# Residual additions of a top-k graph layer and a Mamba layer: from VectorE to identity products in PSUM with ScalarE evictions

## The chip, the cores and the metric

The kernel runs on one core of a Trainium2 chip. The metric is device time in microseconds (us) of one launch. TensorE is written PE (its weight loads PEld), VectorE DVE, ScalarE ACT, GpSimd POOL; SP is the queue from which nearly all DMAs are issued.

## What is computed

x has shape (8, 256, 48, 48): 8 images, 256 channels, 2304 tokens. Two layers follow each other, each with a residual addition around it:

```
x = x + L0(groupnorm(x))     # tokens @ W.T + bias -> feat, pos; pos normalized;
                             # sim = pos pos^T; per token the 16 largest, softmax,
                             # weighted mean of their feat rows
x = x + L1(groupnorm(x))     # two Mamba blocks in a row: layernorm, in-projection,
                             # causal conv of 4 taps, silu, step sizes by softplus,
                             # h = h * exp(dt*A) + dt*B*x (16 states, 512 channels),
                             # y = C.h + D*x, y * silu(z), out-projection
```

These two "x +" are what the change is about. All data are fp32.

## The kernel before, in words

**Layouts.** A chunk is T = 384 tokens; there are NCH = 6 of them in an image, and TB = 3 blocks of 128 tokens in a chunk, so 18 blocks in an image. Activations lie with channels on the 128 partitions (CB = 2 halves of 256 channels).

**The scan sets the order of everything.** A *unit* is one chunk of one Mamba block (depth d = 0 or 1), so there are 12 units in an image and 96 in all; their order within an image, from `order`, is (chunk, depth) = (0,0) (1,0) (2,0) (0,1) (3,0) (1,1) (4,0) (2,1) (5,0) (3,1) (4,1) (5,1), numbered 0 to 11 here. A unit has 16 steps of two parts, so 32 *hooks*; one hook m holds one DVE scan over 770 elements (`run_scan`, L943). For each hook ACT makes two exponentials into one of two PSUM buffers (`decay`, L928). For each step POOL makes the scan's input for all four state groups, 128x1536 (`make_bx`, L907). After the scan its states are multiplied with C either by POOL, once a step for all the parts that fall to it (`pool_part`, L971, issued at the first hook of the next step, 128x1536 for two parts or 128x768 for one), or by DVE at once (L945). Which part goes where is written out by hand in `SHARE`, a string of 32 letters (G for POOL, V for DVE), one string for each of three stages: the middle of an interleaved image (units 1 to 9), its edges (units 0, 10, 11), and the last image. PE then sums the states (`sum_states`, L989).

**Everything else hangs on hooks.** The tables `between`, `behind` and their `_spare` and `_last` forms give for each function of a unit the hook, counted from the unit's first scan, at which it is issued, ahead of that hook's scan (`inner`) or behind it (`outer`). A function of unit u at hook 38 therefore falls in unit u + 1, hook 6. The output projection (`out_proj`, L1005) is at 37 and 38, and `leave` (L1012) at 38 to 40: at depth 0 it copies the projection out of PSUM on ACT (L1020) and stores it; at depth 1 it adds bias and residual on DVE (L1024) and stores the result. The residual was fetched into `res` by `load_out` at hook 33 (L1002).

**Layer 0 of the next image runs between.** `layer0` is a generator. For image 0 it runs alone, before the first scan; for the others `Ahead.go` takes one step of it at each hook, from hook EARLY = -21 before the image's start. First come about 49 steps of projections (`project`, `features`, `norms`, `normalized`, `scale`), then the 18 blocks, 16 hooks apart, whose start is held to a fixed place modulo 16 (L1152). The list `within` (L560) gives the place of each function of a block: similarities on PE, eight largest twice on DVE (`top`), exponentials on ACT, the weighted mean on PE, `average` (22), `turn_back` (24), which transposes the 128x256 result into PSUM with two products by the identity, and `finish` (24), in which DVE adds the transposed result to x (L551). After each third block DVE takes statistics of the chunk and it is stored as x1. The chunk of x for this addition is loaded in `average` of the chunk's first block (L537), into a rotating tile, tag "x", three deep; `load_out` and the projections take their tiles from the same tag.

Each engine works through its instructions in the order in which they are written here, and SP issues its DMAs in that order too, so an instruction or a store that waits holds what is behind it.

The two additions, as they were:

```
nc.vector.tensor_add(xr, xr, row["pr"].rearrange("p (k t) -> p k t", k=CB))        # L551
nc.vector.scalar_tensor_tensor(                                                    # L1024
    res[:, cb, :], unit["pw"][cb], b_feat[:, cb : cb + 1], res[:, cb, :], ALU.add, ALU.add)
```

Of the kernel before, what the change touches and what calls it, by code (L numbers as in the profile page):

```python
# [11 lines left out]
AF = mybir.ActivationFunctionType  # L12
ALU = mybir.AluOpType
# [3 lines left out]
P = 128  # L17
# [9 lines left out]
def tile_conv_preact(  # L27
# [18 lines left out]
    nc = tc.nc  # L46
# [5 lines left out]
    CB = C // P  # L52
# [19 lines left out]
    FOLDED = (2, 3,)  # L72
    EARLY = -21


    SHARE = (
        "GGVGGGVGGGVVGVGGGGGVGGGVGGGGGVVG",
        "GVGGGVVVGGVVGGGGVGGVGGVVVGVVGVGV",
# [8 lines left out]
    def load_chunk(pool, src, c, tag, name, bufs):  # L87
        t = pool.tile([P, CB, T], F32, tag=tag, name=name, bufs=bufs)
        nc.sync.dma_start(t, src[:, c * T : (c + 1) * T].rearrange("(k p) t -> p k t", p=P))
        return t  # L90
# [170 lines left out]
    def layer0(b, left, pool, ps0, alone):  # L261
# [229 lines left out]
        def invert(t):  # L491
            nc.vector.reciprocal(blocks[t]["den"], blocks[t]["den"])

        def others(t, i):
# [36 lines left out]
        def average(t):  # L531
            row = blocks[t]
            row["o"] = pool.tile([P, C], F32, tag="o", name=f"o_{b}_{t}", bufs=more)
            nc.scalar.activation(row["o"], row["po"], AF.Identity, scale=row["den"])
            if t % TB == 0:
                tag, bufs = ("xr", 2) if alone else ("x", 3)
                rows[t // TB] = load_chunk(pool, x[b], t // TB, tag, f"xr_{b}_{t}", bufs)  # L537

        def turn_back(t):
            row = blocks[t]  # L540
            row["pr"] = mm0(C, f"pr_{b}_{t}")
            for cb in range(CB):
                nc.tensor.transpose(
                    row["pr"][:, cb * P : (cb + 1) * P], row["o"][:, cb * P : (cb + 1) * P], ident
                )

        def finish(t):
            row = blocks[t]
            c, j = divmod(t, TB)
            xr = rows[c][:, :, j * P : (j + 1) * P]  # L550
            nc.vector.tensor_add(xr, xr, row["pr"].rearrange("p (k t) -> p k t", k=CB))  # L551
            if j + 1 == TB:
                xr = rows.pop(c)
                for cb in range(CB):
                    nc.vector.bn_stats(st1[:, cb, c, :], xr[:, cb, :])
                nc.sync.dma_start(x1[:, c * T : (c + 1) * T].rearrange("(k p) t -> p k t", p=P), xr)
            row.clear()
# [5 lines left out]
            (16, weigh, 0), (1, top, 1), (-9, similar, 0), (-7, similar, 1), (-7, similar, 2), (22, average),  # L563
            (-6, similar, 3), (-7, keep_similar, 1), (-3, keep_similar, 3), (-1, top, 0),
            (-3, keep_similar, 4), (15, turn, 1), (10, others, 4), (5, others, 0), (3, top, 2), (6, add_top),
# [438 lines left out]
    def out_proj(unit, cb):  # L1004
        pw = unit["pw"][cb] = mm(T, f"pw_{unit['u']}_{cb}")  # L1005
        for k in range(DB):
            nc.tensor.matmul(  # L1007
                pw, unit["ow"][:, k, cb * P : (cb + 1) * P], unit["z"][k],
                start=(k == 0), stop=(k == DB - 1),
            )  # L1010

    def leave(unit, cb):  # L1012
# [9 lines left out]
        else:  # L1022
            res = unit["res"]
            nc.vector.scalar_tensor_tensor(  # L1024
                res[:, cb, :], unit["pw"][cb], b_feat[:, cb : cb + 1], res[:, cb, :], ALU.add, ALU.add
            )
# [25 lines left out]
        (-3, load_rep, "dt", 1), (-29, load_in, 2), (5, in_proj, 7), (-20, tap, 0), (-15, taps, 1),  # L1052
        (-2, load_rep, "dtx", 3), (38, leave, 1), (22, load_rep, "dtx", 15), (-8, load_in, 4), (-37, mean),
        (-19, taps, 0), (5, load_d, 1), (-19, in_proj, 1), (-10, load_bc, 0), (-30, root_end),
        (-9, times_x, 0), (29, gate, 2),
    ]
    between_spare = [
        (25, sum_states, 2), (-34, variance), (-21, in_proj, 0), (38, out_proj, 0), (-15, taps, 2),
        (-35, square), (39, leave, 0), (23, load_rep, "dt", 14), (5, load_rep, "dt", 5),
# [8 lines left out]
        (7, load_rep, "dt", 6), (17, load_rep, "dt", 12), (-6, load_rep, "dtx", 1), (-14, load_in, 7),  # L1068
        (37, gate, 3), (-31, root), (9, load_rep, "dt", 7), (5, load_d, 1), (-24, load_in, 3),
        (17, load_rep, "dt", 11), (14, load_rep, "dtx", 11), (-13, x_proj), (-17, load_in, 6), (-3, load_d, 0),  # L1070
# [8 lines left out]
        (-2, load_rep, "dtx", 3), (8, copy_z, 1), (22, load_rep, "dtx", 15), (-16, load_in, 4), (-38, mean),  # L1079
        (-22, normal), (-37, center), (-21, in_proj, 1), (-12, load_bc, 0), (-30, root_end), (-9, times_x, 0),  # L1080
        (-25, load_in, 1), (-28, scale),
# [9 lines left out]
        (-17, tap, 1), (21, load_rep, "dt", 13), (-20, tap, 0), (-10, step_size, 1), (-5, load_rep, "dt", 0),  # L1091
        (9, copy_z, 2), (-18, in_proj, 2), (2, load_rep, "dtx", 5), (10, sum_states, 0),
        (13, load_rep, "dt", 9), (33, gate, 2), (-2, in_proj, 4), (9, silu_z), (7, load_rep, "dt", 6),
# [125 lines left out]
```

## Time and profile before

| | |
|---|---|
| median of three runs | 9424.92 us (9422.48 to 9425.63) |
| the profiled execution | 9422.82 us |
| its span, first to last instruction | 9421.1 us |
| first scan begins, last scan ends | 468 us, 9409.5 us |
| mean granted PE clock | 0.898 |
| L551, DVE addition in layer 0 | 144 of 407 ns |
| L1024, DVE addition at depth 1 | 96 of 606 ns |
| L1020, ACT copy at depth 0 | 96 of 473 ns |
| L943, DVE scan | 3072 of 1750 ns |
| L907, POOL product | 1536 of 3462 ns |
| L971, POOL product | 669 of 3190 ns (two parts), 648 of 1697 ns (one) |

A group row of the profile gives the line in the kernel, the engine, the operation, out<-in by the program's names, the shapes, the count, the busy time and the mean of one in ns. A row of waits gives who waited (engine, tile, line) for whom, the sum in us, how often, and the longest. A window row gives its bounds, its length and, for each engine, busy time and number of instructions, then the granted PE clock, the DMA share and GB/s. A busy PE is not PE at its peak, since its products overlap.

### The profile page before, as it was taken

What the parts mean: (1) busy time and instruction counts of PE and PEld (TensorE: products, weight loads), DVE (VectorE), ACT (ScalarE), POOL (GpSimd) and SP (SyncE); (2) the same over time, 40 slices, a digit from 0 to 9 for tenths busy, and PEclk for the clock granted to TensorE, in tenths of its full rate; (3) what the DMA queues carried; (4) which work ended last, traced back from release to release, by engine and by line L of the source; (5) the groups of instructions that cost most, each with busy time, mean ns of one, the idle gap of its engine ahead of it and who ended that gap; (6) DMA issues with size and microseconds to landing.
All of it is one profiled execution on the core that took longest, in us unless ns stands there. A gap on an engine that the chain in (4) does not pass through costs nothing. (4 is left out here: it accounts for less than half of the span.)

```text
span 9421.1 us, 120485 instructions
## 1 busy us (share of the span) xinstructions
PE 7867.0 (84%) x37049; PEld 4423.6 (47%) x37049; DVE 8867.3 (94%) x7543; ACT 7307.1 (78%) x16242; POOL 8867.9 (94%) x3605
## 2 busy tenths in 40 slices
PE   8888987888878898798878988788887888877676
PEld 6644544455544554455444545445554455433332
DVE  6599999999989999899999999999999999989999
ACT  4578877788778877787878787778877788777776
POOL 2199999999999999999999999999999999999999
PEclk9989998899989998899988999889998899988877
DMA  4134444444444444444444434443444344444443
GB/s 128 50 123 136 134 137 152 129 136 137 136 151 129 133 140 131 151 131 139 131 144 138 140 128 140 145 138 127 138 134 157 122 141 132 138 153 145 149 147 126
DMA packets 1029829, 1275.91 MB, mean 135 GB/s; under 512 B 106529, under 2 KB 998945, under 8 KB 1028417
## 3 DMA queue, kind: packets, MB, share of 16 engines
q1 hardware_dynamic: 1028640, 1268.21, 42.0%
q8 instruction: 296, 4.85, 0.2%
q14 instruction: 349, 2.85, 0.1%
q10 hardware_dynamic: 544, 0.00, 0.0%
HBM read 1050.77 MB, written 217.06 MB: 135 GB/s over the span
## 5 line engine op out<-in xcount | busy, mean ns | idle before, releaser
L907 POOL TENSOR_TENSOR bx<-BC,dtxr 128x1536 f32<-128x1536 f32 x1536 | 5307.1, 3462 | 33.0 <-PE y L989 30.4
L928 ACT ACTIVATE da<-dtr,A_sb 128x385 f32<-128x385 f32 x6144 | 3592.8, 585 | 928.3 <-DVE bx L943 601.8
L943 DVE TENSOR_TENSOR_SCAN bx<-da,bx 128x770 f32<-128x770 f32 x1986 | 3423.7, 1746 | 85.1 <-ACT da L928 78.7
L971 POOL TENSOR_TENSOR bx<-bx,BC 128x1536 f32<-128x1536 f32 (+1 forms) x1317 | 3233.3, 2455 | 103.7 <-DVE bx L943 91.6
L943 DVE TENSOR_TENSOR_SCAN da<-da,bx 128x770 f32<-128x770 f32 x1086 | 1903.4, 1753 | 125.5 <-ACT da L928 123.1
L527 PE MATMUL po<-feat,aT 128*128 128x256 f32 x5184 | 1378.8, 415 | 236.6 <-ACT dt L842 107.3
L698 PE MATMUL pe<-vn,inw 128*128 128x384 f32 (+1 forms) x2976 | 1175.7, 524 | 216.0 <-ACT vn L775 100.6
L527 PEld LDWEIGHTS po<-feat,aT 128*128 128x128 f32 x5184 | 1022.0, 205 | 633.9 <-ACT aT L516 167.4
L456 PE MATMUL psim<-pos 128*128 128x512 f32 x2520 | 1203.2, 619 | 130.6 <-DVE xr L551 85.4
L989 PE MATMUL y<-bx,sel 128*32 128x384 f32 x12288 | 1221.6, 527 | 72.7 <-POOL bx L971 72.4
L945 DVE TENSOR_TENSOR bx<-da,BC 128x768 f32<-128x768 f32 x1086 | 1040.6, 958 | 37.4
L698 PEld LDWEIGHTS pe<-vn,inw 128*128 128x128 f32 x2976 | 567.6, 201 | 648.0 <-ACT vn L775 125.1
L456 PEld LDWEIGHTS psim<-pos 128*128 128x128 f32 x2520 | 504.4, 209 | 709.8 <-issue 385.3
L989 PEld LDWEIGHTS y<-bx,sel 128*32 128x32 f32 x12288 | 400.5, 117 | 866.6 <-issue 683.2
L803 DVE SCALAR_TENSOR_TENSOR xc<-pe,cw,xc 128x384 f32<-128x384 f32 x1080 | 655.4, 612 | 33.2 <-ACT xc L794 7.8
L516 ACT ACTIVATE aT<-pt 128x512 f32<-128x512 f32 (+1 forms) x720 | 387.7, 547 | 330.9 <-PE pt L508 328.6
L1007 PE MATMUL pw<-z,ow 128*128 128x384 f32 x1536 | 551.0, 505 | 57.5 <-ACT aT L516 38.5
L507 PE MATMUL pt<-ident,sim 128*128 128x128 f32 x2592 | 540.1, 289 | 13.4 <-DVE v L762 5.6
L986 PE MATMUL y<-xc,dmat 128*128 128x384 f32 x768 | 380.7, 581 | 157.7 <-DMA dmat<-diag 43.7
L499 ACT ACTIVATE rest<-left,three 128x512 bf16<-128x512 f32 (+1 forms) x720 | 453.5, 669 | 64.6 <-DVE left L484 64.6
L508 PE MATMUL pt<-minus,rest 128*128 128x128 bf16 x2592 | 496.1, 225 | 3.0 <-ACT rest L499 3.0
L959 ACT COPY h_st<-da 128x2 f32<-128x2 f32 x884 | 138.5, 157 | 419.9 <-DVE bx L945 409.2
(160 smaller groups left out, 9933.9 us busy)
## 6 DMA issues: line engine op xcount, KB each, us to landing
dtxr<-dtx_d SPq DMA_DIRECT2D x1536, 192.0 KB, 2.9
dtr<-dt_d SPq DMA_DIRECT2D x1536, 192.0 KB, 2.8
BC<-bc_d SPq DMA_DIRECT2D x192, 768.0 KB, 5.6
inw<-in_in_wT_dram SPq DMA_DIRECT2D x744, 128.0 KB, 2.5
dtx_d<-dtx SPq DMA_DIRECT2D x384, 192.0 KB, 1.9
dt_d<-dt SPq DMA_DIRECT2D x384, 192.0 KB, 2.0
ow<-in_out_wT_dram SPq DMA_DIRECT2D x96, 512.0 KB, 4.5
dmat<-diag SPq DMA_DIRECT2D x384, 64.0 KB, 2.7
```

The source lines that it names most:

```text
L456: nc.tensor.matmul(pm, pos[:, k, t * P : (t + 1) * P], pos[:, k, c0 : c0 + w], start=(k == 0), stop=(k == CB - 1),)
L507: nc.tensor.transpose(pt[:, q], row["sim"][:, r], ident)
L527: nc.tensor.matmul(row["po"], aT[:, m % PT, :], feat[:, m, :], start=(m == 0), stop=(m == NB - 1))
L698: nc.tensor.matmul(pe, w[:, k], unit["vn"][:, k, lo:], start=(k == 0), stop=(k == CB - 1))
L803: nc.vector.scalar_tensor_tensor(unit["xc"][e], unit["pe"][e][:, k : k + T], cw[:, unit["d"], e, k : k + 1], unit["xc"][e], ALU.mult, ALU.add,
L907: nc.gpsimd.tensor_tensor(bx[:, :, 1:], unit["BC"][0], unit["dtxr"][i].unsqueeze(1).to_broadcast([P, Q, T]), ALU.mult,)
L928: nc.scalar.activation(da[:, s * (1 + T) : (s + 1) * (1 + T)], unit["dtr"][i], AF.Exp, scale=A_sb[:, unit["d"], i, p * HQ + s : p * HQ + s ...
L943: nc.vector.tensor_tensor_scan(h, da, g, 0.0, ALU.mult, ALU.add)
L945: nc.vector.tensor_tensor(bx[:, :, 0:T], da.rearrange("p (q t) -> p q t", q=HQ)[:, :, 1:], unit["BC"][1][:, qs], ALU.mult,)
L971: nc.gpsimd.tensor_tensor(g[:, :, 0:T], g[:, :, 1:], unit["BC"][1][:, qs], ALU.mult)
L989: nc.tensor.matmul(y[j * G : (j + 1) * G, :], sel, unit["bx"][k * J + j][:, q, 0:T], start=False, stop=True, skip_group_check=True,)
L1007: nc.tensor.matmul(pw, unit["ow"][:, k, cb * P : (cb + 1) * P], unit["z"][k], start=(k == 0), stop=(k == DB - 1),)
```

## The change

Both additions are made in PSUM. In `turn_back` each transpose is followed by a product of the identity with the matching 128x128 piece of x, accumulated onto it; in `out_proj`, at depth 1, the four products of each half are followed by a fifth, identity times `res`. ACT then evicts the sum: a copy in `finish`, an Identity activation with the bias column in `leave`. The load of x for layer 0's addition moves from `average` (hook 22 of a block) to `invert` (hook 12). EARLY goes from -21 to -24. In SHARE's first string one V moves from step 6, second part, to step 7, first part. Single entries of the tables move by one to three hooks. The diff, cut to its core:

```diff
-    EARLY = -21
+    EARLY = -24
-        "GGVGGGVGGGVVGVGGGGGVGGGVGGGGGVVG",
+        "GGVGGGVGGGVVGGVGGGGVGGGVGGGGGVVG",
...
         def invert(t):
             nc.vector.reciprocal(blocks[t]["den"], blocks[t]["den"])
+            if t % TB == 0:
+                tag, bufs = ("xr", 2) if alone else ("x", 3)
+                rows[t // TB] = load_chunk(pool, x[b], t // TB, tag, f"xr_{b}_{t}", bufs)
...
             nc.scalar.activation(row["o"], row["po"], AF.Identity, scale=row["den"])
-            if t % TB == 0:
-                tag, bufs = ("xr", 2) if alone else ("x", 3)
-                rows[t // TB] = load_chunk(pool, x[b], t // TB, tag, f"xr_{b}_{t}", bufs)
...
                 nc.tensor.transpose(
                     row["pr"][:, cb * P : (cb + 1) * P], row["o"][:, cb * P : (cb + 1) * P], ident
                 )
+                nc.tensor.matmul(
+                    row["pr"][:, cb * P : (cb + 1) * P], ident,
+                    rows[t // TB][:, cb, t % TB * P : (t % TB + 1) * P],
+                    start=False, stop=True, skip_group_check=True,
+                )
...
-            nc.vector.tensor_add(xr, xr, row["pr"].rearrange("p (k t) -> p k t", k=CB))
+            nc.scalar.copy(xr, row["pr"].rearrange("p (k t) -> p k t", k=CB))
...
-            (-6, similar, 3), (-7, keep_similar, 1), ...
+            (-5, similar, 3), (-7, keep_similar, 1), ...
...
                 pw, unit["ow"][:, k, cb * P : (cb + 1) * P], unit["z"][k],
-                start=(k == 0), stop=(k == DB - 1),
+                start=(k == 0), stop=(k == DB - 1 and "res" not in unit),
             )
+        if "res" in unit:
+            nc.tensor.matmul(pw, ident, unit["res"][:, cb, :], start=False, stop=True)
...
-            nc.vector.scalar_tensor_tensor(
-                res[:, cb, :], unit["pw"][cb], b_feat[:, cb : cb + 1], res[:, cb, :], ALU.add, ALU.add
+            nc.scalar.activation(
+                res[:, cb, :], unit["pw"][cb], AF.Identity, bias=b_feat[:, cb : cb + 1]
             )
...
behind:        (-2 -> -4, load_rep, "dtx", 3)
between_spare: (-34 -> -32, variance), (-31 -> -32, root)
behind_spare:  (-30 -> -31, root_end)
between_last:  (-18 -> -21, in_proj, 2)
```

The last five rows are the moved table entries in short form, with the old and the new hook.

More of the change, by code (lines that the diff above doesn't have):

```diff
@@ L563, in layer0 @@
             (16, weigh, 0), (1, top, 1), (-9, similar, 0), (-7, similar, 1), (-7, similar, 2), (22, average),
-            (-6, similar, 3), (-7, keep_similar, 1), (-3, keep_similar, 3), (-1, top, 0),
+            (-5, similar, 3), (-7, keep_similar, 1), (-3, keep_similar, 3), (-1, top, 0),
             (-3, keep_similar, 4), (15, turn, 1), (10, others, 4), (5, others, 0), (3, top, 2), (6, add_top),
@@ L1052, in tile_conv_preact @@
         (-3, load_rep, "dt", 1), (-29, load_in, 2), (5, in_proj, 7), (-20, tap, 0), (-15, taps, 1),
-        (-2, load_rep, "dtx", 3), (38, leave, 1), (22, load_rep, "dtx", 15), (-8, load_in, 4), (-37, mean),
+        (-4, load_rep, "dtx", 3), (38, leave, 1), (22, load_rep, "dtx", 15), (-8, load_in, 4), (-37, mean),
         (-19, taps, 0), (5, load_d, 1), (-19, in_proj, 1), (-10, load_bc, 0), (-30, root_end),
@@ L1057, in tile_conv_preact @@
     between_spare = [
-        (25, sum_states, 2), (-34, variance), (-21, in_proj, 0), (38, out_proj, 0), (-15, taps, 2),
+        (25, sum_states, 2), (-32, variance), (-21, in_proj, 0), (38, out_proj, 0), (-15, taps, 2),
         (-35, square), (39, leave, 0), (23, load_rep, "dt", 14), (5, load_rep, "dt", 5),
@@ L1068, in tile_conv_preact @@
         (7, load_rep, "dt", 6), (17, load_rep, "dt", 12), (-6, load_rep, "dtx", 1), (-14, load_in, 7),
-        (37, gate, 3), (-31, root), (9, load_rep, "dt", 7), (5, load_d, 1), (-24, load_in, 3),
+        (37, gate, 3), (-32, root), (9, load_rep, "dt", 7), (5, load_d, 1), (-24, load_in, 3),
         (17, load_rep, "dt", 11), (14, load_rep, "dtx", 11), (-13, x_proj), (-17, load_in, 6), (-3, load_d, 0),
@@ L1079, in tile_conv_preact @@
         (-2, load_rep, "dtx", 3), (8, copy_z, 1), (22, load_rep, "dtx", 15), (-16, load_in, 4), (-38, mean),
-        (-22, normal), (-37, center), (-21, in_proj, 1), (-12, load_bc, 0), (-30, root_end), (-9, times_x, 0),
+        (-22, normal), (-37, center), (-21, in_proj, 1), (-12, load_bc, 0), (-31, root_end), (-9, times_x, 0),
         (-25, load_in, 1), (-28, scale),
@@ L1091, in tile_conv_preact @@
         (-17, tap, 1), (21, load_rep, "dt", 13), (-20, tap, 0), (-10, step_size, 1), (-5, load_rep, "dt", 0),
-        (9, copy_z, 2), (-18, in_proj, 2), (2, load_rep, "dtx", 5), (10, sum_states, 0),
+        (9, copy_z, 2), (-21, in_proj, 2), (2, load_rep, "dtx", 5), (10, sum_states, 0),
         (13, load_rep, "dt", 9), (33, gate, 2), (-2, in_proj, 4), (9, silu_z), (7, load_rep, "dt", 6),
```

## The prediction

> **What bounds the kernel now.** I read in this order: busy time by engine, the windows of one image cut at its 12 units (one unit is 32 scans; I took the starts of scans 0, 32, 64 ... from the timeline), the waits of POOL, and the timeline at one of them.
>
> ```profile
> PE 7867.0 (84%) x37049; PEld 4423.6 (47%) x37049; DVE 8867.3 (94%) x7543; ACT 7307.1 (78%) x16242; POOL 8867.9 (94%) x3605
> ```
>
> DVE and POOL are level at 94%, and both lose most of the rest in the first 468 us (image 0's layer 0, before the first scan), so an average cannot say which sets the pace. The windows can. Units 2 to 9 of image 3 (columns: window, its length, busy PE, PEld, DVE, ACT, POOL):
>
> ```profile
> 4255.10:4352.00 96.90, 83.77 (x409) 47.22 (x408) 95.44 (x81) 78.56 (x177) 95.03 (x36) 0.95 0.43 139
> 4352.00:4447.40 95.40, 87.58 (x412) 49.86 (x411) 94.47 (x81) 77.71 (x177) 95.40 (x36) 0.91 0.41 131
> ...
> sum 763.80, PE 675.97 PEld 384.83 DVE 755.19 ACT 619.20 POOL 759.64; mean PE 84.50 PEld 48.10 DVE 94.40 ACT 77.40 POOL 94.96
> ```
>
> In unit 5 POOL has no gap at all (95.40 of 95.40); in unit 4 it loses 1.87 us. Over the eight units POOL is idle 763.80 - 759.64 = 4.2 us, DVE 8.6. So here **POOL is the floor**, and DVE can only give back what POOL waits for it. All of that wait is one row:
>
> ```profile
> POOL bx L971 <- DVE bx L943: 91.6, 64, 3.3
> POOL bx L907 <- PE y L989: 30.4, 32, 2.6
> ```
>
> In order of time the 91.6 us lie so: units 1, 2, 4, 6, 8 of the seven interleaved images 17, 3, 12, 11 and 6, each time at hook 16 (the multiply of step 7); unit 0, 33 (hooks 13 and 22); the last image 9. The cause at hook 16 of unit 4 is to be seen ten hooks earlier, on DVE:
>
> ```profile
> 4273.70 1.14 DVE L1024 SCALAR_TENSOR_TENSOR xr<-pw,b_feat,xr 128x384 f32<-128x384 f32 x2 [0.80 <-PE pw L1007]
> 4304.10 3.17 POOL L971 TENSOR_TENSOR bx<-bx,BC 128x1536 f32<-128x1536 f32 x1 [1.87 <-DVE bx L943]
> ```
>
> The two residual additions and the wait ahead of them take 1.94 us of DVE, and POOL then waits 1.87. Unit 5, where the same place holds a depth-0 eviction on ACT, has no such wait. That pair is the experiment the change repeats.
>
> **What the Trainium skill says.** "SBUF — State Buffer", section "Who interferes with whom": a DVE instruction with at most one SBUF input does not contend with GpSimd. Both additions read one operand in PSUM, so removing them should not make POOL's own instructions shorter. The trace agrees loosely: the 128x1536 product of L907 is 3462 ns in the mean, 3442 in the last image where no L551 runs. "ScalarE: Activation LUTs", "What ACT_TABLE_LOAD costs": a pointer operand adds about 93 ns; here a 128x384 copy from PSUM takes 473 ns (L1020) and one with a bias column 575 (L369). "TensorE: Matmul & The Clock Gate", Part 2: ScalarE is strict FIFO, so an eviction that waits for PE holds the decays behind it; L1020 shows it (78.9 us in 42 waits).
>
> **The change, part by part.** Base: the profiled execution, 9422.82 us (span 9421.1 and 1.7 around it); the median 9424.92 is 2.1 above.
>
> 1. *finish* off DVE: 144 x 407 ns (L551) = 59 us of DVE gone. ACT gains 144 x 0.37 (L378, 128x256 copy from PSUM, 364 ns) = 53. PE gains two identity products a block. An fp32 product is two recorded passes (L1007: 1536 records for 96 x 2 x 4 products); a 128-column pass starts every 0.11 us (six of L446 in 0.82 against four in 0.61), so 4 x 0.11 = 0.44 a block, 64 us in all. Wait on ACT: at hook 30 PE has finished pr 3.5 us before ACT gets there; at hook 14 it ends 0.4 us after the decay, plus 0.44, so 0.85. Queued behind: the next decay and DVE's scan, which has 0.66 us to spare there; DVE is 0.41 earlier itself. Net nothing, up to 0.5 us a block; below nothing too, since PE's psim waits 85.4 us for L551 to free its bank and ACT would free it up to 5 us sooner, but PE is not the floor.
> 2. *leave* off DVE: 96 x 606 ns = 58 us, and its waits for pw, 23.6. ACT gains 96 x 575 = 55. PE gains 96 x 2 x 0.32 = 62. In units 4, 6, 8 both evictions come while out_proj is still running: ACT waits as its L1020 does in unit 5 (1.7) plus two passes, 2.4 us. Behind it are the decay of hook 8 and, on DVE, its scan; DVE has a 2.54 us MATCH_REPLACE at hook 7 to cover it, and unit 5 shows no DVE gap. If that cover went, 2.4 - 1.9 = 0.5 us a unit. In units 10, 11 and 0 PE is done 3 to 5 us early, so no wait, but 2 x 0.575 = 1.1 us of ACT work lands just before silu_z (two table loads of 1.28 and four activations), whose burst already starves DVE at hooks 10 to 13. POOL has 1.2 to 3 us in hand there in units 10 and 11 (its multiply starts that long after the scan it needs) but 0.1 in unit 0.
> 3. *SHARE*: one V moves from step 6 to step 7 of the middle stage. Counts stay (8 GG, 7 mixed, 1 VV), so POOL's sum stays. But step 6 becomes a 3190 ns multiply in place of 1697: POOL has 1.5 us more to do ahead of hook 16, where it now waits. In unit 1 (wait 2.4) it must first wait about 1.3 for the later scan of step 6; 1.1 is won.
> 4. The *xr load* moves 10 hooks earlier, past the loads of some five steps on SP's queue. It takes 3.8 us to land and its buffer (3 deep) was left long before; the identity product needs it at hook 24, 12 hooks (35 us) later. At the old place only two hooks (6 us) would remain. The *res* load leads by four hooks (12 us) against 5.2. The stores wait for ACT now, which arrives 2 to 5 us earlier than DVE did: nothing lost.
> 5. *EARLY* -24 and the table rows: layer 0's projections come three hooks sooner; the blocks keep their hooks (their start is fixed modulo 16, and at -21 they started without slack). In unit 0 two position evictions, with 2.4 us of waits for PE, move out of hooks 7 and 8, ahead of the burst. In unit 11 a 1.4 us normalization moves to hook 9, into it. From -2 to +2 us an image; I take -1.5. The single moves in the tables (root, variance, a load, an input projection) shift DMA issues and short ACT work by one to three hooks: nothing, +-5 us in all.
>
> The sum:
> - Units 1 to 9: waits of 3 + 12 + 11 + 6 = 32 us in units 2, 4, 6, 8 go, since DVE sheds 1.6 us in each unit and 1.9 more in 4, 6 and 8, ahead of the wait; unit 1 gives 7 x 1.1 = 8. 40 us at best. POOL is next late: it has nothing left to give. A tenth comes back in new waits on later decays: **-36**.
> - Units 10, 11: 0. Unit 0: 7 x (1.1 - 1.5) = **-3**.
> - Last image: POOL sits at its floor (L971's wait for scans is 9 us over 12 units) with DVE idle some 5 us a unit: 0; its tail ends in one more product and a 575 ns eviction in place of 606: **+1**.
> - The first 468 us: PE is busy 47 of 50 us in most windows, so 18 x 0.44 = 8 at most; DVE's 0.41 a block is beside the path there. **+6**.
> 9422.8 - 36 - 3 + 1 + 6 = 9391; less sure of the first term than of the rest, and with 126 us more work on a PE that is 84 to 92% busy in the middle units, I allow 5 back: 9396.
>
> **Rivals.**
> - *ACT's queue takes over (slower).* In units 4, 6, 8 ACT's added time is 2.4 + 1.1 = 3.5 against 1.9 that DVE sheds; per block 0.85 + 0.37 and 0.37 against 0.8 for the two in a unit. If every ACT delay reaches DVE's next scan and then POOL: 3 x 1.6 + 9 x 0.8 + 3 x 1.1 = 15 us an image, 105 in seven. It decides from where ACT's lag passes the 0.4 to 0.7 us that decays have in hand at hooks 14 and 30. For it: the decay is the last thing DVE waits for (202 us). Against: ACT is idle 17 to 22 us a unit, and unit 5. Half of it, less half the gain: 9423 + 52 - 18 + 7 = **9464**.
> - *The gain is given back at the image boundary.* Unit 0 loses 8 to 9 us of POOL a unit already; if its burst grows by 1.1 + 2 and unit 11's reserve of 2.5 is used up too, 7 x 4 = 28 us return: 9396 + 28 = **9424**. For it: 0.1 us in hand. Against: the waits for PE that leave hooks 7 and 8.
> - *The boundary gets better as well*: if moving the projections clears most of unit 0's POOL waits (33 + 19 us), say 25 us: **9371**.
> - *Nothing because POOL does not wait for DVE* (the releaser is inferred) is ruled out by unit 4 against unit 5.
>
> **Chances.** Forecast (9380 to 9412) 0.55; boundary better 0.13; given back 0.14; ACT takes over 0.18. About 0.2% (19 us, 9406) is what a measurement of this kernel can tell from no change. Faster: 0.13 and nine tenths of 0.55 less a little, 0.61. Same: the rest of it and 0.14, 0.20. Slower: 0.18 and the upper edge of the third, 0.19. The range runs from the better boundary to a little over the midway of the slow case: 9366 to 9445; the forecast's own is 9380 to 9412.
>
> **What would show it.** Right: the row "POOL bx L971 <- DVE" falls from 92 to some 45 us, with units 4, 6, 8 as long as 5 and 7 (95), POOL's busy time unchanged within 0.2%, DVE down by about 115 us and its waits for ACT's decays up. Wrong: POOL's gaps move to other hooks; DVE's wait for da doubles within units 2 to 9; unit 0 longer than 98 us; the first scan more than 8 us later; or POOL's products getting shorter, which I exclude.

## The result, and the profile after

| | before | after |
|---|---|---|
| median of five runs | 9425.63 us (9422.48 to 9431.65) | 9387.33 us (9386.1 to 9391.59) |
| the profiled execution, its span | 9422.82, 9421.1 us | 9387.99, 9385.9 us |
| first scan begins | 468.0 us | 476.4 us |

The ratio is 0.9959 (95% interval 0.9945 to 0.9974), 38 us less. The prediction was 9396, with a range of 9366 to 9445. The total came out as forecast. Where the gain lies did not.

Busy time by engine in the changed kernel:

```profile
PE 7960.8 (85%) x37817; PEld 4514.8 (48%) x37817; DVE 8771.5 (93%) x7303; ACT 7382.4 (79%) x16482; POOL 8867.3 (94%) x3605
```

POOL's sum is the old one (8867.9) to 0.01%; DVE has lost 96 us, ACT and PE have gained 75 and 94. In the windows of units 4, 5, 6 and 8 of image 3, cut at their scans as in the prediction (PE, PEld, DVE, ACT, POOL, then the granted clock), and the sum over units 2 to 9:

```profile
4240.85:4336.18 95.33, 85.51 (x419) 49.22 (x418) 93.76 (x78) 79.33 (x181) 94.99 (x36) 0.95 0.44 142
4336.18:4430.47 94.29, 86.19 (x425) 49.46 (x423) 93.63 (x78) 78.05 (x179) 94.29 (x35) 0.96 0.40 129
4430.47:4525.32 94.85, 85.23 (x422) 49.65 (x422) 92.96 (x75) 79.24 (x182) 94.85 (x36) 0.96 0.43 139
...
4620.20:4715.64 95.44, 87.84 (x427) 50.65 (x425) 93.80 (x77) 75.77 (x157) 95.44 (x37) 0.95 0.41 134
...
sum 761.38, PE 682.62 PEld 393.89 DVE 747.15 ACT 625.28 POOL 759.79; mean PE 85.33 PEld 49.24 DVE 93.39 ACT 78.16 POOL 94.97
```

Unit 4 was 96.90 us and is 95.33, close to unit 5. POOL is idle 1.6 us in the eight units (4.2 before), while DVE is idle 14.2 (8.6 before): DVE has become looser, POOL is the floor all the more. POOL's waits, which were 91.6 for scans and 30.4 for PE:

```profile
POOL nt_rn L176 <- ACT rn L168: 39.6, 17, 4.7
...
POOL bx L976 <- DVE bx L948: 32.1, 56, 1.9
```

The wait for scans has lost 60 us, more than forecast (to 45), but above it stands a row that the prediction has nowhere: a 9-element POOL operation that waits for ACT.

**Where the 35 us of span went.** In the loop, from the first scan to the end of the last, all that POOL does besides waiting takes 8783.5 us before and 8784.0 after. So the length of the loop is this constant and POOL's idle time, and the change can be booked by where that idle time lies. I summed the idle stretch ahead of each POOL instruction, over the seven interleaved images, by the unit in which it ends (units are cut at DVE's scans, and POOL carries work across these cuts, so neighbouring units can trade some of it):

| POOL idle, us | units 0, 1 | 2 to 9 | 10, 11 | last image | sum | POOL active | first scan |
|---|---|---|---|---|---|---|---|
| before | 89.1 | 34.7 | 24.0 | 10.0 | 157.8 | 8783.5 | 468.0 |
| after | 62.1 | 9.1 | 30.1 | 11.5 | 112.8 | 8784.0 | 476.4 |

The loop is 45 us shorter. The first stage gives 8.4 back and the tail behind the last scan 1.1: 35. Only 26 of the 45 lie in units 2 to 9, where both removed additions and the new SHARE string should act. 27 come from the two units at the start of each image, and there the windows of image 3 show it; before (units 0 and 1):

```profile
3873.09:3970.30 97.21, 79.13 (x362) 45.59 (x363) 85.58 (x77) 74.72 (x172) 88.00 (x43) 0.85 0.42 132
3970.30:4065.19 94.89, 79.59 (x340) 40.66 (x339) 93.02 (x76) 75.36 (x171) 90.37 (x34) 0.86 0.40 128
```

and after:

```profile
3861.18:3955.15 93.97, 77.13 (x352) 44.67 (x350) 84.60 (x74) 73.82 (x168) 85.22 (x37) 0.86 0.42 136
3955.15:4048.78 93.63, 79.87 (x341) 40.66 (x341) 92.67 (x76) 74.58 (x171) 93.63 (x36) 0.89 0.42 131
```

Unit 0 is 3.2 us shorter, and in unit 1 POOL now never stops (93.63 of 93.63), where it lost 4.5.

### The profile page after: what moved, and what is told of

Its sections match the earlier page's. It is cut to its first block, busy times and chain, and to the rows that moved or that the text cites. A ratio compares the mean times of both kernels' runs of the same rounds, so it can differ in the third digit from the quotient of the medians.

```text
span 9385.9 us, 121932 instructions
## 1 busy us (share of the span) xinstructions
PE 7960.8 (85%) x37817; PEld 4514.8 (48%) x37817; DVE 8771.5 (93%) x7303; ACT 7382.4 (79%) x16482; POOL 8867.3 (94%) x3605
## 5 line engine op out<-in xcount | busy, mean ns | idle before, releaser
L912 POOL TENSOR_TENSOR bx<-BC,dtxr 128x1536 f32<-128x1536 f32 x1536 | 5297.7, 3455 | 18.0 <-PE y L994 16.3
L994 PE MATMUL y<-bx,sel 128*32 128x384 f32 x12288 | 1261.1, 528 | 102.5 <-POOL bx L976 97.2
L703 PE MATMUL pe<-vn,inw 128*128 128x384 f32 (+1 forms) x2976 | 1140.7, 510 | 157.7 <-ACT vn L780 60.0
L456 PE MATMUL psim<-pos 128*128 128x512 f32 x2520 | 1124.0, 590 | 68.0 <-ACT xr L556 25.9
L950 DVE TENSOR_TENSOR bx<-da,BC 128x768 f32<-128x768 f32 x1086 | 1040.7, 958 | 37.5
L994 PEld LDWEIGHTS y<-bx,sel 128*32 128x32 f32 x12288 | 406.1, 116 | 931.0 <-issue 680.2
L703 PEld LDWEIGHTS pe<-vn,inw 128*128 128x128 f32 x2976 | 543.9, 194 | 573.8 <-ACT vn L780 79.8
L838 PE MATMUL pd<-dbl,dtp_sb 16*128 16x384 f32 x768 | 362.6, 614 | 136.3 <-DVE z L1000 66.2
```

Source lines behind the costliest of these rows:

```text
L456: nc.tensor.matmul(pm, pos[:, k, t * P : (t + 1) * P], pos[:, k, c0 : c0 + w], start=(k == 0), stop=(k == CB - 1),)
L703: nc.tensor.matmul(pe, w[:, k], unit["vn"][:, k, lo:], start=(k == 0), stop=(k == CB - 1))
L912: nc.gpsimd.tensor_tensor(bx[:, :, 1:], unit["BC"][0], unit["dtxr"][i].unsqueeze(1).to_broadcast([P, Q, T]), ALU.mult,)
L950: nc.vector.tensor_tensor(bx[:, :, 0:T], da.rearrange("p (q t) -> p q t", q=HQ)[:, :, 1:], unit["BC"][1][:, qs], ALU.mult,)
L994: nc.tensor.matmul(y[j * G : (j + 1) * G, :], sel, unit["bx"][k * J + j][:, q, 0:T], start=False, stop=True, skip_group_check=True,)
```

## The experiments

Two theories stood against each other. **DVE relief**: the gain is the prediction's first term, DVE work taken away ahead of POOL's waits. **Boundary**: it is EARLY, which moves the projections out of the way at the start of each image, and the additions themselves bring little. All runs stand here in the terms of the table above, with their ratio to the kernel before. EARLY, the depth-1 addition and the SHARE string were each tried alone and undone in the changed kernel; layer 0's addition was tried alone, and undone together with the other one (early24_share). The moved table entries were never tried apart: they are in every after_ run, in first_image_dve, one_more_v and norm_end_later, and in none of the others.

| run | units 0, 1 | 2 to 9 | 10, 11 | sum | first scan | median us | ratio (95%) |
|---|---|---|---|---|---|---|---|
| before_early24 | 51.4 | 30.5 | 34.4 | 126.2 | 468.1 | 9389.92 | 0.9961 (0.9947 to 0.9975) |
| before_finish | 88.6 | 19.1 | 21.2 | 140.1 | 476.9 | 9418.39 | 0.9990 (0.9983 to 0.9997) |
| before_leave | 96.2 | 14.5 | 22.0 | 144.2 | 471.9 | 9418.62 | 0.9992 (0.9984 to 1.0001) |
| before_share | 89.2 | 23.7 | 25.5 | 148.2 | 471.0 | 9415.78 | 0.9990 (0.9983 to 0.9996) |
| after_early21 | 86.7 | 6.2 | 19.2 | 124.0 | 477.9 | 9399.72 | 0.9972 (0.9962 to 0.9982) |
| after_early23 | 61.5 | 6.6 | 38.0 | 115.9 | 477.3 | 9395.80 | 0.9968 (0.9957 to 0.9980) |
| after_leave_dve | 53.2 | 7.7 | 30.1 | 101.1 | 477.4 | 9377.24 | 0.9949 (0.9932 to 0.9965) |
| after_old_share | 62.5 | 9.2 | 30.9 | 114.1 | 475.7 | 9394.27 | 0.9969 (0.9957 to 0.9981) |
| early24_share | 47.1 | 23.4 | 35.5 | 115.8 | 467.4 | 9384.25 | 0.9958 (0.9943 to 0.9973) |
| first_image_dve | 53.6 | 5.7 | 31.3 | 100.7 | 469.1 | 9368.99 | 0.9941 (0.9926 to 0.9955) |
| one_more_v | 64.7 | 98.9 | 30.7 | 203.8 | 468.9 | 9384.15 | 0.9958 (0.9943 to 0.9973) |
| norm_end_later | 45.3 | 8.1 | 30.4 | 93.6 | 470.5 | 9362.34 | 0.9936 (0.9919 to 0.9952) |

POOL's active time is 8782 to 8789 us in all of them but one_more_v. The stage before the first scan moves by 3 to 4 us by itself: before_share and before_leave change nothing in it. Each row of idle time is one profiled execution. The intervals are 6 to 16 us to either side, so a smaller difference between two medians is only as good as the idle time that goes with it.

### EARLY alone, and taken back

before_early24, the kernel before with one number changed:

```diff
-    EARLY = -21
+    EARLY = -24
```

> The kernel before with EARLY -24 alone. In the changed kernel -24 against -21 made unit 0 22 us shorter (seven images) while POOL waited 33 us at hook 19. If that comes from the position evictions that leave hooks 7 and 8, it shows here too: unit 0 shorter by 15 to 22 us, 9402 to 9411. If it only repairs what the eviction of depth 1 on ACT did to the burst, it gives under 5 us here: 9420 to 9426.

It takes 29.4 us off the span, and its median is within 3 us of the whole change: more than either outcome that was expected. Its windows of units 0 and 1:

```profile
3863.31:3955.13 91.82, 72.75 (x347) 41.46 (x346) 85.58 (x77) 72.83 (x165) 85.20 (x37) 0.87 0.43 140
3955.13:4050.03 94.90, 79.51 (x340) 40.43 (x339) 93.02 (x77) 75.38 (x171) 94.18 (x36) 0.88 0.40 128
```

Part of it lies ahead of silu_z's burst of table loads on ACT. In unit 0 of the kernel before, which starts at 3873.09, two position evictions wait for PE, and the first table load follows 28.5 us into the unit:

```profile
3894.71 0.58 ACT L369 ACTIVATE pos<-pp,b_pos 128x384 f32<-128x384 f32 x1 [1.33 <-PE pp L342]
...
3898.58 0.58 ACT L369 ACTIVATE pos<-pp,b_pos 128x384 f32<-128x384 f32 x1 [0.98 <-PE pp L342]
...
3901.56 1.28 ACT L867 ACT_TABLE_LOAD   x1
```

With EARLY at -24 the unit starts at 3863.31, these two evictions are gone from that place, and the same load is at 25.9 us:

```profile
3889.20 1.28 ACT L867 ACT_TABLE_LOAD   x1
```

Image 3 flatters this: over the seven images the load comes at 27.4 us before and at 26.3 with EARLY at -24, 1.1 us sooner. The larger part lies behind the burst. There, in the kernel before, three evictions of features (L378) and a normalization (L307) stand between the decays, and DVE waits for the decays of scans 11, 12 and 13:

```profile
3905.89 0.37 ACT L378 COPY feat<-pf 128x256 f32<-128x256 f32 x1
...
3908.92 0.36 ACT L378 COPY feat<-pf 128x256 f32<-128x256 f32 x1
...
3910.61 0.36 ACT L378 COPY feat<-pf 128x256 f32<-128x256 f32 x1
3910.87 1.31 ACT L307 ACTIVATE xt<-xt,shift_a,rstd_a 128x384 f32<-128x384 f32 x2
```

```profile
3907.40 1.77 DVE L943 TENSOR_TENSOR_SCAN da<-da,bx 128x770 f32<-128x770 f32 x1 [1.40 <-ACT da L928]
...
3910.69 1.76 DVE L943 TENSOR_TENSOR_SCAN bx<-da,bx 128x770 f32<-128x770 f32 x1 [0.53 <-ACT da L928]
3913.49 1.76 DVE L943 TENSOR_TENSOR_SCAN bx<-da,bx 128x770 f32<-128x770 f32 x1 [1.04 <-ACT da L928]
```

With EARLY at -24 a 0.26 us activation for the norms (L385) and one position eviction stand there in their place, and DVE goes through two of the scans without a stop:

```profile
3893.53 0.26 ACT L385 ACTIVATE n<-pn,tiny 128x3 f32<-128x3 f32 x1
...
3897.86 0.58 ACT L369 ACTIVATE pos<-pp,b_pos 128x384 f32<-128x384 f32 x1
```

```profile
3894.92 1.77 DVE L943 TENSOR_TENSOR_SCAN da<-da,bx 128x770 f32<-128x770 f32 x1 [0.88 <-ACT da L928]
...
3897.94 3.58 DVE L943 TENSOR_TENSOR_SCAN bx<-da,bx 128x770 f32<-128x770 f32 x2 [0.25 <-ACT da L928]
```

These three waits fall from 3.0 us an image to 1.2, and scan 16 starts 3.3 us sooner after the start of its unit (47.0 to 43.6, means of seven). POOL, which had waited for such scans at hooks 13 and 22 (33 us over seven images), waits 10 at hook 13 and nothing at 22; its 19 us of waits for PE's sums (L989) at hooks 3 to 18 shrink to 2. In the kernel before, POOL's idle stretches in units 0 and 1 (scans late in three of them):

```profile
3915.39 3.18 POOL L971 TENSOR_TENSOR bx<-bx,BC 128x1536 f32<-128x1536 f32 x1 [3.28 <-DVE bx L943]
...
3940.74 3.16 POOL L971 TENSOR_TENSOR bx<-bx,BC 128x1536 f32<-128x1536 f32 x1 [2.13 <-DVE bx L943]
...
4017.27 3.17 POOL L971 TENSOR_TENSOR bx<-bx,BC 128x1536 f32<-128x1536 f32 x1 [2.17 <-DVE bx L943]
```

and with EARLY at -24:

```profile
3901.66 3.17 POOL L971 TENSOR_TENSOR bx<-bx,BC 128x1536 f32<-128x1536 f32 x1 [1.49 <-DVE bx L943]
...
3921.46 0.20 POOL L176 TENSOR_TENSOR nt_rn<-rn 128x9 f32<-128x9 f32 x1 [4.74 <-ACT rn L168]
...
4002.10 3.17 POOL L971 TENSOR_TENSOR bx<-bx,BC 128x1536 f32<-128x1536 f32 x1 [0.72 <-DVE bx L943]
```

The last of each is the wait at hook 16 of unit 1, which the prediction gave to the additions and SHARE. EARLY alone takes it from 17 us in seven images to 5. The line in the middle is the likely reason: the new wait at hook 19 (32 us) puts POOL later, and a later POOL finds its scans done. Two runs without that wait agree: unit 1 idles 16 us in after_early23 and 22 in norm_end_later (below), and nothing in the changed kernel. before_finish, before_leave and before_share leave unit 1 at 31, 31 and 28 us of idle time (31 before).

The changed kernel with EARLY taken back:

```diff
-    EARLY = -24
+    EARLY = -21     (after_early21; -23 in after_early23)
```

> The changed kernel with EARLY back at -21, all else as changed. If the earlier projections won in unit 0 by taking the position evictions out of hooks 7 and 8, unit 0 loses that: its POOL waits at hook 13 return with 1.1 us of leave on ACT on top, 3 to 4.5 us an image, but the hook 19 wait of 4.7 us goes: net within 10 us of the changed kernel, 9380 to 9397. If -24 did nothing for hooks 7 to 13, the time falls by the whole hook 19 wait, to 9355 to 9365.

> The changed kernel with EARLY -23 in place of -24: all of layer 0's projection steps one hook later. In the changed kernel POOL waits 33 us at hook 19 of unit 0 (4.7 us in each of seven images) for ACT's first half of the inverse norm, which at -24 is issued behind silu_x at hook 18. If that wait is real loss of POOL's time (POOL is the floor there), it goes or shrinks to under 1.5 us an image, unit 0 gets 2 to 4 us shorter and the kernel 15 to 30 us faster than the changed one, some 9360 to 9372. If unit 0 is bound by ACT's burst at hooks 9 to 13 and not by POOL, POOL's wait goes and the time stays at 9387 within 6.

At -21 the changed kernel is 12 us slower, 3 us past the range expected: units 0 and 1 lose 25 (87 against 62), units 10 and 11 get 11 back, since the projections that EARLY takes out of unit 0 arrive in unit 11, and units 2 to 9 get 3. At -23, where 15 to 30 us less were expected, it is 8 us slower than the change. The wait at hook 19 falls to some 4 us, but waits elsewhere in units 0 and 1 take its place (their sum stays at 61.5), and units 10 and 11 lose 8 us more: two hooks give the start of the image all it gains, and the third spares unit 11.

So neither theory holds alone. By medians, each against that of the kernel before taken with it, EARLY by itself takes 37 us, everything but EARLY (after_early21) takes 26, and both together take 38. Their gains overlap: EARLY is worth 32 us of idle time on the kernel before and 11 in the changed one.

### Each addition alone, and the SHARE string

before_finish makes only layer 0's addition in PSUM (load of x in `invert`, identity product in `turn_back`, `nc.scalar.copy` in `finish`), before_leave only the one at depth 1 (fifth product in `out_proj`, activation in `leave`), before_share only the string:

```diff
-        "GGVGGGVGGGVVGVGGGGGVGGGVGGGGGVVG",
+        "GGVGGGVGGGVVGGVGGGGVGGGVGGGGGVVG",
```

> The kernel before with only layer 0's addition moved to PSUM and ACT (its load moved to hook 12 with it); depth 1's addition, SHARE, EARLY and the tables as before. If what POOL waits for at hook 16 is DVE's whole load of the units, 0.65 us less of DVE a unit (two additions at their spacing of 0.32) takes 25 to 35 of the 50 us: units 1 to 9 shorter by 25 to 35, the first stage 8 longer, 9398 to 9408. If it is the additions of depth 1 just ahead of the wait, hook 16's waits in units 4, 6, 8 stay over 20 us and only unit 1's and 2's go: 9415 to 9428.

> The kernel before with only depth 1's addition moved to PSUM and ACT. My prediction's step: units 4, 6, 8 lose their waits (29 us), unit 0 loses 8 to 10 us to ACT's burst: 9400 to 9410. The rival, after the last runs: POOL's waits in 4, 6, 8 go, but PE's 0.64 us and ACT's 0.575 us for each half come back as waits in the units after them and in units 0, 10, 11, so that less than 10 us remain: 9415 to 9430.

> The kernel before with only the first string of SHARE changed (one V from step 6 to step 7). If POOL waits at hook 16 because it has too little work between steps 5 and 7, part of the 50 us goes: up to 1.5 us in each of units 1, 2, 4, 6, 8 where it waits, less what the later scan of step 6 costs in unit 1: 8 to 35 us faster, 9390 to 9417. If DVE sets the pace in units 1 to 9 (no slack on DVE), filling POOL's gap moves its wait to another hook and gains nothing: 9420 to 9426.

Each takes away POOL's idle time in units 2 to 9, most of it the wait at hook 16 of units 4, 6 and 8: 15.6, 20.2 and 11.0 us, 47 together, where only 34.7 were to be had and the change got 25.6. That is what a floor looks like: three remedies for one wait, and any one of them would have taken a third to over a half. None is worth much alone: before_finish loses 8.9 us ahead of the first scan, before_leave 7 in unit 0, before_share has new waits at hooks 13, 18 and 28, and the medians of all three lie 7 to 10 us below that of the kernel before, at the edge of what the intervals can tell. before_finish's median lies in the second range expected of it, but not for its reason: the waits at hook 16 of units 4, 6 and 8 fell from 29 us to 13, and it is unit 1's that stayed.

The string was then taken out of the changed kernel (the diff above reversed):

> The changed kernel with the old first SHARE string: the only part that no run has undone in the changed kernel. Alone on the kernel before, the new string took about 10 us in units 1 to 9 of seven images; finish alone about 20, the depth-1 addition alone about 23, and the three together 34.5, which is what POOL lost there. Theory of the saturated floor: either of the other two parts alone already covers most of units 4, 6 and 8, so the string is worth only what it saves in units where neither helps, unit 1 above all (17 us of waits at hook 16 that finish alone left standing): 5 to 12 us longer than the changed kernel, 9392 to 9399, with the wait at hook 16 back in unit 1 and none in units 4, 6 and 8. Rival: with both additions off DVE the string no longer matters, or its new waits at hooks 13 and 28 cost as much as it saves: within 4 us of 9387. Second rival: the parts add up, and the string's 10 us come back in units 4, 6 and 8 as well: 9397 or more.

The idle time is 114.1 against 112.8, and unit 1 doesn't wait: by idle time the string brings nothing any more. The expectation looked for the wait in unit 1 and was wrong on the place, since EARLY had already covered it. The median of six runs is 6.9 us higher all the same, and in the profiled one POOL's active time is 5 us longer (8789.0), for which the trace gives no cause; the intervals of the two ratios overlap. What the string is worth in the changed kernel, between nothing and 7 us, stays open.

early24_share puts the two cheap edits together, with both additions left on DVE:

```diff
-    EARLY = -21
+    EARLY = -24
-        "GGVGGGVGGGVVGVGGGGGVGGGVGGGGGVVG",
+        "GGVGGGVGGGVVGGVGGGGVGGGVGGGGGVVG",
```

> The kernel before with EARLY -24 and SHARE's new string: nothing is moved to PSUM. It tells what the additions are worth beside those two. If layer 0's additions on ACT are what units 1 to 9 of the changed kernel owe their gain to, this stays 12 to 20 us above first_image_dve: 9380 to 9390, with POOL's waits at hooks 16 to 28 of units 2 to 8 over 15 us. If SHARE alone would do, it reaches 9367 to 9375.

9384.25 us against the change's 9387.33: with neither addition moved the kernel is as fast, within what the intervals tell. In units 2 to 9 it is 14 us worse (23.4 against 9.1); it has that back in units 0 and 1 (15) and in the first stage (9), and gives 5 away in units 10 and 11.

### The depth-1 addition undone

after_leave_dve has `out_proj` and `leave` as they were, and all else changed.

```diff
-        if "res" in unit:
-            nc.tensor.matmul(pw, ident, unit["res"][:, cb, :], start=False, stop=True)
...
-            nc.scalar.activation(
-                res[:, cb, :], unit["pw"][cb], AF.Identity, bias=b_feat[:, cb : cb + 1]
+            nc.vector.scalar_tensor_tensor(
+                res[:, cb, :], unit["pw"][cb], b_feat[:, cb : cb + 1], res[:, cb, :], ALU.add, ALU.add
             )
```

> The changed kernel with the depth-1 addition back on DVE and without its identity product; finish, SHARE, EARLY and the load stay changed. If the two additions and the wait ahead of them in units 4, 6, 8 are what POOL waited for, 1.9 us each comes back on DVE; SHARE's 1.5 us reserve takes part of it: 5 to 30 us slower than the changed kernel, units 4, 6, 8 longer by 0.3 to 1.5. If the middle of the image is POOL's alone now and SHARE did the work, no difference there, and units 0, 10, 11 get shorter by up to 1.1 us each for ACT's lighter burst: up to 15 us faster.

It is 10 us faster than the change; the slowest of its four runs, 9379.54, is below the fastest of the change, 9386.1. Units 2 to 9 are no worse (7.7 against 9.1), although DVE has 45 us more to do; units 0 and 1 are 8.9 better. With finish on ACT, EARLY and the string the second relief has nothing left to relieve there, and its cost stays. The run takes back the product on PE and the eviction on ACT together, so which of the two costs more isn't shown: in the changed kernel ACT waits 61.5 us for L1017 and has 1.15 us more work in unit 0 ahead of the burst, while 7.7 of the 8.9 us are POOL's waits for PE's sums (L994) at hook 10 of unit 0, 9.4 against 1.7; before_leave has them too, 12.1 against 2.7 before.

The waits of ACT that the prediction priced are there at about their size. Timeline of ACT in the changed kernel, image 3, unit 4:

```profile
4260.72 0.58 ACT L1031 ACTIVATE xr<-pw,b_feat 128x384 f32<-128x384 f32 x1 [2.37 <-PE pw L1017]
...
4285.02 0.37 ACT L556 COPY xr<-pr 128x256 f32<-128x256 f32 x1 [0.63 <-PE pr L546]
```

2.37 us against 2.4 forecast, 0.63 against 0.85. And DVE does wait more for decays, by group row (idle before, in the last columns, was 123.1 and 78.7 in the kernel before):

```profile
L948 DVE TENSOR_TENSOR_SCAN bx<-da,bx 128x770 f32<-128x770 f32 x1986 | 3422.8, 1746 | 122.7 <-ACT da L933 102.5
...
L948 DVE TENSOR_TENSOR_SCAN da<-da,bx 128x770 f32<-128x770 f32 x1086 | 1904.2, 1753 | 166.7 <-ACT da L933 165.0
```

Most of the growth lies in units 2 to 9, where these waits rise from some 5 to 46 us over seven images, while POOL's idle time there falls to 9.1.

### Image 0 left on DVE

first_image_dve is after_leave_dve with layer 0 of image 0, which runs alone, as it was:

```diff
+                if not alone:
                     nc.tensor.matmul(
                         row["pr"][:, cb * P : (cb + 1) * P], ident,
...
+            if alone:
+                nc.vector.tensor_add(xr, xr, row["pr"].rearrange("p (k t) -> p k t", k=CB))
+            else:
                 nc.scalar.copy(xr, row["pr"].rearrange("p (k t) -> p k t", k=CB))
```

> The changed kernel with depth 1's addition back on DVE, and image 0's layer-0 addition too (no identity products there); the other seven images' layer-0 additions stay in PSUM and on ACT. If PE bounds the first stage, the first scan begins 7 to 9 us earlier than in the changed kernel, as before the change, and the time is that of the kernel with only depth 1 on DVE (9377) less that: 9366 to 9372. If the first stage is longer for another reason (order of the work, the load), the time stays at 9374 to 9380.

The first scan is back at 469.1 from 477.4, and the median 8.3 us lower. Five runs with the product in image 0 start their scans at 475.7 to 477.9 (six with the changed kernel), those without at 467.4 to 471.9. The 8 us are those that the prediction had for PE's products, 18 x 0.44, as a bound. The run takes back the products and ACT's copy together, so that they are PE's is argued from their size and from a PE that is busy most of that stage.

### Is there room on DVE?

In units 2 to 9 DVE is idle 1.8 us a unit in the changed kernel (image 3) and 1.4 in first_image_dve (seven images); one more part moved from POOL to DVE costs DVE 0.96 (L950) and takes 1.5 from POOL, the floor. one_more_v does that to first_image_dve:

```diff
-        "GGVGGGVGGGVVGGVGGGGVGGGVGGGGGVVG",
+        "GGVGGVVGGGVVGGVGGGGVGGGVGGGGGVVG",
```

> first_image_dve with one more V in SHARE's first string (step 2, second part: a POOL multiply of 3190 ns becomes one of 1697, and DVE gains one of 958, 875 at its spacing). If POOL is the floor in units 1 to 9 and DVE has its 1 to 2 us of idle a unit to spare, each of the 63 units gets 0.5 to 1 us shorter: 9310 to 9340. If DVE and POOL are level now, DVE's 0.875 us a unit becomes the pace: nothing or up to 20 us slower, 9365 to 9390, with POOL's waits for scans over 60 us.

It is 15 us slower. POOL's active time falls by 87, as it should, but its idle time rises by 103. POOL's wait for scans in first_image_dve:

```profile
POOL bx L980 <- DVE bx L952: 29.2, 40, 1.9
```

and in one_more_v:

```profile
POOL bx L980 <- DVE bx L952: 118.1, 155, 3.3
```

The new waits are mostly at hooks 13 and 28 of units 1 to 9. For this place of the V, the idea that DVE has room to spare is refuted: what a sum over a unit shows as idle on DVE is not there ahead of the scans that POOL needs. Another place, or the changed kernel itself with some 50 us less on DVE, was not tried.

### The new wait at hook 19

norm_end_later, on first_image_dve, lets two more hooks pass before POOL takes the root that it waits for (`inverse_norm_end` of the last chunk); the blocks keep their hooks:

```diff
         inverse_norm(NCH - 1)
         yield
+        yield
+        yield
         inverse_norm_end(NCH - 1)
```

> The kernel with depth 1's addition and image 0's on DVE (first_image_dve, 9369), with POOL's half of the last inverse norm two steps of layer 0 later (hook 21 in place of 19 of unit 0; the blocks keep their hooks). POOL waits 32 us at hook 19 for ACT's half, which stands behind silu_x. If that is POOL's own loss, it goes and units 0 and 1 get 20 to 32 us shorter: 9337 to 9349. If unit 0's length is set by DVE and ACT there, POOL only waits elsewhere and the time stays at 9364 to 9372.

Its median lies between the two ranges expected, near the second. The 32 us at hook 19 are gone, and 22 of them come back as waits in unit 1 (hooks 2, 4, 13 and 28). Its windows of units 0 and 1:

```profile
3849.55:3944.46 94.91, 76.64 (x350) 43.68 (x348) 85.56 (x77) 72.78 (x166) 89.99 (x39) 0.86 0.42 134
3944.46:4037.66 93.20, 79.28 (x346) 42.06 (x345) 92.57 (x76) 74.56 (x171) 90.07 (x34) 0.86 0.41 133
```

POOL gets more done in unit 0 (89.99) and has then less to do in unit 1, where it waits again. The net is 6.6 us, a fifth of the wait that was taken away, and the ranges of the two versions' runs overlap (to 9368.66, from 9367.55): at the start of an image POOL waits for the others in one place or another. It has the lowest median of all, 9362.34 us, 25 below the change.

## Why the prediction came out right

**The sum holds term by term in the order in which it was made**, with EARLY last. The measured column is POOL's idle time over the seven images and what the two ends cost: everything but EARLY is after_early21 against the kernel before, EARLY is the change against after_early21.

| term | forecast, us | measured, us |
|---|---|---|
| units 1 to 9 | -36 | -40 |
| unit 0, the depth-1 addition (7 x 1.1) | +8 | +9 |
| units 10, 11 | 0 | -5 |
| last image and tail | +1 | +3 |
| first stage | +6 | +10 |
| EARLY (7 x -1.5) | -10.5 | -11 |

The forecasts add up to -32, the measured terms to -34; the 5 us that the prediction allowed back on top were not needed. No term is off by more than 5 us, in single executions, so read in this order the total is not luck. Of the first term, 28.5 us come in units 2 to 9 and 11.6 in unit 1, where 29 and 7 were said; units 4, 6 and 8 end as long as 5 and 7 (in the change 95.6, 94.8 and 95.0 against 94.5 and 95.1, means of seven images), and POOL, the floor, gives nothing more. The first scan is 8.4 us later in the change, past the 8 that the prediction named as a sign against it.

**What the prediction had wrong is that its terms add up in any order.** EARLY alone, put at 10 us, takes 32 of idle time; then the rest wins 21 us in units 2 to 9 and 4 in units 10 and 11, loses 11 in units 0 and 1 and 11 at both ends, and nets 3 us in the medians, where the prediction's terms for it (-36, +8, +1, +6) make -21. The overlap is largest in unit 1: of its 31 us of idle time EARLY alone takes 26, the rest alone 12, both together 31. And "DVE sheds 1.6 us in each unit and 1.9 more" is more than units 2 to 9 need: with finish, EARLY and SHARE the depth-1 addition adds nothing there (after_leave_dve), and costs 8.9 us in unit 0.

**Step 5, EARLY: the size is right, partly by luck, and the reason is only a part of it.** "I take -1.5" is a choice out of a range from -2 to +2, with no sum behind it. Measured on top of the rest, EARLY wins 25 us in units 0 and 1 and loses 11 in units 10 and 11 and 3 in units 2 to 9. The loss lies where step 5 saw a 1.4 us normalization arrive, in unit 11, and is about of that size (1.6 us an image); "Units 10, 11: 0" leaves it out.

The gain was to come from "two position evictions, with 2.4 us of waits for PE", that no longer stand ahead of the burst; but the burst comes only 1.1 us sooner with EARLY alone and 0.3 in the changed kernel (28.5 to 28.2 us into the unit, means of seven). More is won behind it, where DVE's waits at scans 11 to 13 fall from 3.0 us an image to 1.2 (to 1.6 in the changed kernel), and 19.5 of the 25 us lie in unit 1, which step 5 doesn't have. The new wait at hook 19, 33 us, is in no term. How much of the gain each moved step brings was read from timelines, not tried apart. The rival in which "the boundary gets better as well", put at .13, asked for 25 us: that is what units 0 and 1 give, but units 10 and 11 take part of it back, and the total stays in the forecast's own range.

**The rival on ACT's queue** ended on the other side. Its sign came: DVE's waits for decays in units 2 to 9 did far more than double, which the prediction had named as a sign of its being wrong. That test was badly chosen. DVE has those waits in time that POOL, the floor, doesn't need; only a wait of POOL behind them would have counted.

**Smaller points.** DVE fell by 96, not by 115. An addition's record overlaps the next instruction: L551 lasts 407 ns by its record, but the next instruction starts 323 ns after it; L1024 606 and 523. 144 x 0.323 + 96 x 0.523 = 96.7. On ACT the records overlap as well: L556 and L1031 last 365 and 572 ns, but the next instruction starts 264 and 475 ns after them when it doesn't wait; 144 x 0.264 + 96 x 0.475 = 84, where 108 was said and 75 measured. PE gained 94 where 126 was said, which is not explained. The mean of L907's product in the last image is 3451 ns, not 3442. POOL's products stayed as they were, as "SBUF — State Buffer", "Who interferes with whom", of the Trainium skill lets one expect when a DVE operation with at most one SBUF input (L551 has one, besides its PSUM operand) is taken away: active time 8783.5 and 8784.0 us.

## What to carry to other kernels

When one engine is the floor, book a change in that engine's idle time, by stage: the sum of it and of a constant is the time, and several remedies for the same wait add up only until it is gone. What a part is worth then depends on what is already there: time each part of a change alone and taken back. Here one constant alone gives almost the whole gain, everything else without it gives two thirds, and half of the headline edit is a loss once the rest is in. Work that is moved to another engine costs where that engine has its burst, so price it there, and look behind the burst as well as ahead of it.

## What was not expected of the hardware

- A POOL instruction's recorded duration can move while its pace doesn't: the mean record of the 128x1536 product is 3462 ns before, 3455 after and 3497 in first_image_dve, but POOL's active time in the loop is 8783.5, 8784.0 and 8785.3 us, and when the next POOL instruction follows without a gap, it starts 3406 to 3407 ns after the product in all three. Records overlap their successors, so a difference of one per cent in such a mean is not a faster or slower engine. For DVE the Trainium skill says as much ("Perfetto Trace Analysis", "Optimizing Scalar/DVE Operations": the write acknowledgement overlaps the next instruction); here it is 83 to 84 ns for L551 and L1024.
- POOL waited 4.7 us an image, 33 in all, ahead of a 9-element operation of 0.20 us; taking the wait away won 6.6 us (norm_end_later). Its input, a root on ACT, stood behind silu_x with its two table loads of 1.28 us and DVE's convolution. ACT's timeline in the changed kernel:

```profile
3914.73 1.28 ACT L814 ACT_TABLE_LOAD   x1
3916.03 1.35 ACT L816 ACTIVATE xc<-xc 128x384 f32<-128x384 f32 x3
3919.03 0.52 ACT L816 ACTIVATE xc<-xc 128x384 f32<-128x384 f32 x1 [1.65 <-DVE xc L808]
3919.57 1.28 ACT L817 ACT_TABLE_LOAD   x1
...
3921.20 0.21 ACT L168 ACTIVATE rn<-rn 128x9 f32<-128x9 f32 x1
```
